# A two-layer graph network: the first layer's output product with node sums stationary, and the second edge sum's products one tile earlier

## The chip, the cores and the metric

The kernel runs on one core of a Trainium2 chip. The metric is the device time of one launch in microseconds (us), the median of several runs. The core has five engines, each with its own instruction queue that runs in order: PE (TensorE, matrix products and transposes into PSUM), DVE (VectorE), ACT (ScalarE), POOL (GpSimd) and SP (SyncE, which only issues DMAs here). They wait for each other through semaphores. PEld in the profile is PE's loading of the stationary operand, which overlaps with products.

## The reference

Inputs: x (128 graphs, 128 nodes, 64 features), adj (128 x 128 x 128, about an eighth of the entries positive, the rest zero), and weights W1 (128 x 192), b1, W2 (192 x 64), b2, W (64 x 64), all float32. Cut to what is computed:

```python
def _L0_gnn_ref(x, adj, W1, b1, W2, b2):
    mask = (adj > 0.0).astype(x.dtype)
    W1a, W1b = (W1[:F], W1[F:])
    xj_proj = x @ W1a
    diff = x[:, :, None, :] - x[:, None, :, :]
    h = jax.nn.relu(xj_proj[:, :, None, :] + diff @ W1b + b1)
    hm = jnp.einsum('bjkh,bjk->bjh', h, mask)
    deg = jnp.sum(mask, axis=-1)
    return hm @ W2 + deg[..., None] * b2

def _L1_gnn_ref(vertices, g_mat, W):
    agg = jnp.einsum('bnm,bmf->bnf', g_mat, vertices)
    return jnp.einsum('bnf,of->bno', agg, W)

h = jnp.maximum(_layernorm(x, axis=-1), 0.0)
x = x + _L0_gnn_ref(h, adj, W1, b1, W2, b2)
h = jnp.maximum(_layernorm(x, axis=-1), 0.0)
return x + _L1_gnn_ref(h, adj, W)
```

For each graph b and node j, hm[j] is the sum over j's neighbours k of relu(A[j] - C[k]), with 192 hidden units. hm @ W2 is the product that the change rewrites.

## The kernel before

**Groups.** The 128 graphs are handled in 32 groups of four (G = 4). In a group, graph b is written as b = 2p + r, p and r in 0 and 1. The first 128 hidden units are "kind 0" (one graph fills the 128 partitions), the other 64 are "kind 1" (two graphs, p = 0 and 1, share the partitions).

**Slots and edges.** A node's neighbours are put into 24 slots (four quarters of the neighbours, six slots each). One-hot matrices S pick the neighbour of a slot, and PE forms A[j] - C[k] for all slots in PSUM (`Job.fill`, tile g). For kind 0, DVE sums absolute values over the slots (tile hm; relu(x) is half of x + |x|, and the linear halves are put in elsewhere). For kind 1, ACT takes the relu (tile T) and POOL adds the slots up. Nodes with more neighbours in a quarter than slots have the rest on a list of up to 128 edges (tiles ov, R, S2, X, RT), which is subtracted or added by `edge_sum` and `edge_sum1`.

**Tiles in time.** A group has T = 24 jobs, called tiles 0 to 23 here, in the hand-written ORDER: 0 to 3 kind 0, 4 and 5 kind 1, 6 to 9 kind 0, 10 and 11 kind 1, and the same once more for r = 1. Products of kind 0 use the whole 128-column array, those of kind 1 use it as two halves of 64 columns. Behind each tile the tables AHEAD, OWN and BEHIND (lines 909 to 936) hang other work: AHEAD is the preparation of group g + 1 (its slots, ranks, the projections pp at tiles 7 and 12, the edge lists), OWN the edge values X, BEHIND the end of group g - 1. Before the change BEHIND reads:

```python
0: (slot_sum,), 1: (edge_sum,), 4: (edge_sum1,), 8: (post0,), 10: (post1,),
15: (post2,), 16: (post3,), 19: (post4,),
```

At one tile BEHIND stands ahead of AHEAD.

**The end of a group.** `slot_sum` adds the two halves of hm0 on POOL (hs). `edge_sum` forms pe0 in PSUM and u0 = hs - pe0 on DVE: u0 is [128 hidden, 4 graphs, 128 nodes]. `edge_sum1` does the same for the other 64 units: two transposes of z1, eight records of products X by RT with 64-column halves, and u1 = hm1 - pe1 on DVE, [2 x 64 hidden, r, 128 nodes]. `post0` multiplies with W2 as the stationary operand, so that the result py has output features on partitions; ACT copies it to ys. `post1` transposes ys back (pty), adds the residual e on DVE to form x1 (the first layer's output, nodes on partitions; the profile calls it x), and takes mean and variance of each graph (four bn_stats and four bn_aggr on DVE, tiles stb and mvb). `post2` is the second layer norm (ACT: square root sdb, four h; DVE: rsb, mrb), `post3` the product with adj (pga, copied to agg by ACT), `post4` the product with W (po), the sum with x1 on DVE (ot) and the store.

**Projections.** `pre_proj` forms pp (float) on PE, and ACT copies it to bf16 (ca<-pp), then writes z (four instructions) and e (two). DVE takes what the rounding left (rest), ACT rounds that (ca<-rest), POOL the last remainder; DMAs then stack the three parts for the next group (k3).

**Edge weights on ACT.** For each group ACT computes R in nine instructions: four et<-iov,mid, four et<-et,half (pre_edge_b), and R itself.

**PSUM.** The tiles g and pp share three buffers of two banks (ps_g), all other products two buffers of one bank (ps_m). A new tile waits for the readers of the tile whose buffer it takes.

**What sets the order.** PE's instructions stay in the order of the program throughout (`mm` and `tp`). For DVE, ACT, POOL and SP only the start of the kernel is held (Engine.held); from group 0 on a scheduler in the tile layer sorts each engine's instructions when the program is built, by its own estimate of when they are ready. The order on each engine is then fixed.

Of the kernel before, what the change touches and what calls it, by code (L numbers as in the profile page):

```python
# [8 lines left out]
F32 = mybir.dt.float32  # L9
BF16 = mybir.dt.bfloat16  # L10
I32 = mybir.dt.int32
AF = mybir.ActivationFunctionType
ALU = mybir.AluOpType
# [137 lines left out]
def kernel(  # L151
# [28 lines left out]
    def mm(*args, **kw):  # L180
        return tc.keep_in_program_order(nc.tensor.matmul(*args, **kw))  # L181

    def tp(*args, **kw):
        return tc.keep_in_program_order(nc.tensor.transpose(*args, **kw))  # L184

    class Engine:
# [4 lines left out]
        def __init__(self, engine):  # L191
            self.engine = engine
# [10 lines left out]
    vec, act, pool, sp = (Engine(e) for e in (nc.vector, nc.scalar, nc.gpsimd, nc.sync))  # L203

    B, N, F = x.shape
    H = W1.shape[1]
    O = W2.shape[1]
    P = 128
    G = 4
# [18 lines left out]
    with ExitStack() as main:  # L228
# [4 lines left out]
        tmp = main.enter_context(tc.tile_pool(name="tmp", bufs=2))  # L233
# [3 lines left out]
        def gtile(name):  # L237
            return ps_g.tile([P, 2, 512], F32, tag="g", name=name)

        def mtile(name):  # L240
            return ps_m.tile([P, 512], F32, tag="m", name=name)
# [7 lines left out]
        w2bd = const.tile([P, 2, O], F32, tag="w2bd", name="w2bd")  # L249
        wl1 = const.tile([P, P], F32, tag="wl1", name="wl1")  # L250
        ident = const.tile([P, P], F32, tag="ident", name="ident")
# [20 lines left out]
        for q in range(Q):  # L272
            s = slice(q * QN, (q + 1) * QN)
# [35 lines left out]
        w2h = const.tile([C0, O], F32, tag="w2h", name="w2h")  # L309
# [69 lines left out]
        def bc(t, n, axis):  # L379
            shape = list(t.shape)  # L380
            shape.insert(axis, n)
            return t.unsqueeze(axis).to_broadcast(shape)
# [37 lines left out]
        def keep_busy(tile, n):  # L420
            for _ in range(n):
                mm(tile, oneb, bc(oneb, 4, 1), start=True, stop=True, skip_group_check=True)

        def pre_adj(g, busy=0):
            d = groups[g]
            pt = mtile(f"pt{g}")
            keep_busy(pt, busy)
            for b in range(G):
                tp(pt[:, b * N : (b + 1) * N], d["adj"][:, b, :], ident)
            d["adjT"] = grp.tile([P, G, N], F32, tag="adjT", name=f"adjT{g}", bufs=3)  # L430
            if g == 0:
                pre_norm(0)
            act.activation(
                d["adjT"].rearrange("k b j -> k (b j)"), pt, AF.Copy
            )
            if g < 2:
                return
            pre_mask(g)
# [11 lines left out]
            d["h"] = tmp.tile([P, 2, 2, F], F32, tag="h", name=f"h{g}", bufs=1)  # L450
            norm_b(d["x"], d["mv"], lambda b: d["h"][:, b % 2, b // 2, :], f"a{g}", d.get("scales"))

        def pre_rank(g, busy=0):
            d = groups[g]
            pq = mtile(f"pq{g}")
            keep_busy(pq, busy)
            mm(
                pq, triq, d["maskT"].rearrange("k b j -> k (b j)"), start=True, stop=True
            )
            d["qs"] = grp.tile([P, G, N], BF16, tag="qs", name=f"qs{g}")  # L460
            qf = d["qs"].rearrange("k b j -> k (b j)")
            act.activation(qf, pq, AF.Copy)

            d["ov"] = grp.tile([P, G, N], BF16, tag="ov", name=f"ov{g}")
            vec.tensor_scalar(d["ov"], d["qs"], float(D) + BIG, None, ALU.is_ge)
# [56 lines left out]
                d["hT"].rearrange("p r n -> p (r n)"), ph[:, 0 : 2 * N], AF.Copy  # L522
            )

        def pre_count(g, busy=0):
            d = groups[g]

            pd = mtile(f"pd{g}")
            keep_busy(pd, busy)
            for b in range(G):  # L530
                mm(
                    pd[:, b : b + 1], d["maskT"][:, b, :], negb, start=True, stop=True
                )
                mm(
                    pd[:, G + b : G + b + 1], d["ov"][:, b, :], oneb[:, 0:1], start=True, stop=True
                )
            d["dn"] = grp.tile([P, 2, G], F32, tag="dn", name=f"dn{g}")
            vec.tensor_copy(d["dn"].rearrange("j t b -> j (t b)"), pd[:, 0 : 2 * G])

            d["ns"] = grp.tile([P, G], F32, tag="ns", name=f"ns{g}")  # L540
            vec.scalar_tensor_tensor(
                d["ns"], pd[:, G : 2 * G], float(Q * D), d["dn"][:, 0], ALU.add, ALU.subtract
            )

            d["half"] = tmp.tile([P, G], F32, tag="half", name=f"half{g}")
            vec.tensor_scalar(
                d["half"], pd[:, G : 2 * G], -0.5, 0.5, ALU.mult, ALU.add
            )
            d["nb"] = tmp.tile([P, G], BF16, tag="nb", name=f"nb{g}")
            vec.tensor_copy(d["nb"], pd[:, G : 2 * G])  # L550
# [197 lines left out]

        def edge_sum1(g):
            d = groups[g]  # L750
            ph = mtile(f"pe1{g}")
            for r in range(2):
                mm(
                    ph[:, r * N : (r + 1) * N], d["z1"][:, r].rearrange("j p u -> j (p u)"), ident,
                    start=r == 0, stop=False, is_transpose=True, skip_group_check=True,
                )
            for b in (0, 2, 1, 3):
                p, r = b // 2, b % 2
                mm(
                    ph[p * C1 : (p + 1) * C1, r * N : (r + 1) * N], d["X"][:, b, C0:H],  # L760
                    d["RT"][:, b, :], start=False, stop=True, skip_group_check=True,
                )
            d["u1"] = tmp.tile([P, 2, N], F32, tag="u1", name=f"u1{g}", bufs=1)
            vec.tensor_tensor(
                d["u1"], d["hm1"], ph[:, 0 : 2 * N].rearrange("h (r j) -> h r j", r=2), ALU.subtract
            )


        def post0(g):
            d = groups[g]  # L770
            py = mtile(f"py{g}")
            d["py"] = py
            for p in range(2):
                s = slice(p * O, (p + 1) * O)
                mm(
                    py[s, 0 : 2 * N], w2h,
                    d["u0"][:, 2 * p : 2 * p + 2].rearrange("h r j -> h (r j)"),
                    start=True, stop=False, skip_group_check=True,
                )
            w = w2bd.rearrange("h p o -> h (p o)")  # L780
            mm(
                py[:, 0 : 2 * N], w, d["u1"].rearrange("h r j -> h (r j)"),
                start=False, stop=True, skip_group_check=True,
            )
            d["ys"] = tmp.tile([P, 2, N], F32, tag="ys", name=f"ys{g}", bufs=1)
            act.activation(
                d["ys"].rearrange("p r j -> p (r j)"), py[:, 0 : 2 * N], AF.Copy
            )

        def post1(g):  # L790
            d = groups[g]
            pt = mtile(f"pty{g}")
            for r in range(2):
                tp(pt[:, r * N : (r + 1) * N], d["ys"][:, r], ident)
            d["x1"] = grp.tile([P, G, F], F32, tag="x1", name=f"x1{g}")
            vec.tensor_tensor(
                d["x1"].rearrange("j (p r) o -> j r p o", p=2),
                pt[:, 0 : 2 * N].rearrange("j (r p o) -> j r p o", r=2, p=2),
                d["e"].rearrange("j (p r) o -> j r p o", p=2),
                ALU.add,  # L800
            )
            d["mv"] = norm_a(d["x1"], f"b{g}")

# [30 lines left out]


        class Job:
            def __init__(self, g, kind, b, jh, qp, busy):
                self.g, self.kind, self.b, self.jh, self.qp = g, kind, b, jh, qp
                self.gt = gtile(f"g{g}_{kind}_{b}_{jh}_{qp}")
                keep_busy(self.gt[:, 0], busy)  # L840

                if kind == 0:
                    self.parts = [(b, slice(0, C0), slice(0, P))]
                else:
                    self.parts = [
                        (2 * p + b, slice(C0, H), slice(p * C1, (p + 1) * C1)) for p in range(2)
                    ]
# [79 lines left out]
        BEHIND = {  # L927
            0: (slot_sum,),
            1: (edge_sum,),
            4: (edge_sum1,),  # L930
            8: (post0,),
            10: (post1,),
            15: (post2,),
            16: (post3,),
            19: (post4,),
# [85 lines left out]
        for g in range(NG):  # L1021
            if 0 < g < NG - 1:
                load(g + 1)
            order = ORDER0 if g == 0 else ORDERL if g == NG - 1 else ORDER
            for t, args in enumerate(order):
                job = Job(g, *args, busy=0)
                job.fill()
                job.drain()
                if g == 0 and t in FIRST:
                    FIRST[t](0)  # L1030
                pieces(OWN, t, g)
                pieces(BEHIND, t, g - 1)
                pieces(AHEAD if g else AHEAD0, t, g + 1)
# [37 lines left out]
```

## Time and profile before

| what | us |
|---|---|
| runs shown: median (lowest to highest) | 972.44 (972.28 to 972.99) |
| the profiled execution: its own time | 972.88 |
| its span, first to last instruction | 971.2 |
| one group in the steady part | 29.13 |
| first rank product of group 1, and of group 31 | 15.2, 903.9 |
| mean granted TensorE clock | 0.994 |

A line of the timeline has start, length, engine, source line, operation, the tiles that it writes and reads by name, their shape, how many instructions are merged in the line, and in brackets how long the engine was idle before it and what ended that. For PE, "128*128" is the stationary operand and "128x256" the moving one or the result; a float product is recorded as two records, a bf16 product as one. Nearly all instructions carry the line of a helper (L181 for products, L184 for transposes, L198 for the other engines), so tiles are found by name.

Some groups of the profile that the change touches (count, busy us in all, mean ns of one):

| engine, tiles | form | count | busy | mean |
|---|---|---|---|---|
| PE py<-u,w2h | 128*64, 256 columns, float | 128 | 20.8 | 404 |
| PE py<-u,w2bd | 128*128, 256 columns, float | 64 | 22.4 | 431 |
| PE pty<-ident,ys | 128*128 transposes | 64 | 13.9 | 299 |
| ACT ys<-py | 128x256 | 32 | 13.5 | 422 |
| DVE x<-pty,e | 128x256 | 32 | 13.3 | 416 |
| DVE stb<-x | 128x64 | 128 | 19.4 | 213 |

### The profile page before, as it was taken

The numbers are of one execution on the slowest core, as the hardware profiler recorded it, in microseconds if no ns is written. First come the engines' busy times: TensorE is split into PE (matmuls) and PEld (weight loads), VectorE is DVE, ScalarE is ACT, GpSimd is POOL, SyncE is SP. The second block draws the span as 40 slices with busy tenths as digits, with TensorE's granted clock in tenths as the row PEclk, the third lists the DMA queues.
The fourth block names the chain that finished last, engine by engine and source line by source line (L and its number), as shares of the span: only waits on it lengthen the run. The fifth ranks groups of instructions, "written<-read, shape, count | busy, mean of one in ns | idle before, by whom it ended". The sixth has DMA issues, their size and how long they took to land. (4 is left out here: it accounts for less than half of the span.)

```text
span 971.2 us, 26764 instructions
## 1 busy us (share of the span) xinstructions
PE 945.9 (97%) x10007; PEld 692.5 (71%) x10008; DVE 796.4 (82%) x1880; ACT 698.9 (72%) x1732; POOL 743.1 (77%) x1130
## 2 busy tenths in 40 slices
PE   6899999999999999999999999999999999999995
PEld 2667777777777767777777777777777777777774
DVE  6788888888888888888888888888888888888863
ACT  4867787767787767787767787767787767787752
POOL 1388787778787778787778787778787778787793
PEclk9999999999999999999999999999999999999998
DMA  3655676655676655676655676655676655666510
GB/s 99 132 128 126 150 166 137 148 128 124 145 165 144 138 127 128 147 163 144 138 128 128 146 163 137 145 129 127 146 164 144 140 126 126 147 154 138 123 46 14
DMA packets 88294, 129.91 MB, mean 134 GB/s; under 512 B 47200, under 2 KB 63968, under 8 KB 88160
## 3 DMA queue, kind: packets, MB, share of 16 engines
q1 hardware_dynamic: 87584, 127.98, 57.8%
q8 instruction: 81, 1.33, 0.6%
q14 instruction: 53, 0.43, 0.1%
q10 hardware_dynamic: 576, 0.16, 0.1%
HBM read 13.01 MB, written 4.19 MB: 18 GB/s over the span
## 5 line engine op out<-in xcount | busy, mean ns | idle before, releaser
L198 POOL TENSOR_TENSOR T<-T 128x192 f32<-128x192 f32 (+2 forms) x768 | 526.3, 692 | 97.2 <-ACT T L198 57.2
L198 DVE TENSOR_REDUCE hm<-g 128x64 f32<-128x768 f32 x512 | 476.8, 947 | 81.2 <-PE g L181 79.5
L181 PEld LDWEIGHTS <-k 96*128 96x128 bf16 (+1 forms) x6144 | 411.0, 103 | 177.1 <-issue 51.3
L181 PE MATMUL g<-S,k 96*128 96x384 bf16 (+1 forms) x2048 | 381.9, 330 | 4.7 <-DVE hm L198 3.5
L181 PE MATMUL g<-id,k 96*128 96x192 bf16 (+1 forms) x4096 | 379.8, 246 | 0.0
L198 ACT ACTIVATE T<-g 128x768 f32<-128x768 f32 x256 | 209.5, 820 | 74.5 <-PE g L181 70.2
L198 POOL TENSOR_TENSOR ca<-rest,ca 128x384 bf16<-128x384 f32 x126 | 112.5, 913 | 103.7 <-ACT ca L198 101.2
L198 ACT ACTIVATE ca<-pp 128x768 bf16<-128x768 f32 x64 | 51.4, 803 | 56.0 <-PE pp L181 56.0
L198 DVE TENSOR_TENSOR rest<-pp,ca 128x768 f32<-128x768 f32 x64 | 60.8, 949 | 14.6 <-ACT e L198 14.0
L198 ACT ACTIVATE ca<-rest 128x768 bf16<-128x768 f32 x64 | 55.2, 862 | 22.2 <-DVE rest L198 22.2
L198 DVE TENSOR_SCALAR S<-qs 128x512 bf16<-128x512 bf16 x186 | 71.0, 434 | 0.0
L181 PE MATMUL pe<-RT,X 128*64 128x128 f32 (+1 forms) x512 | 70.5, 280 | 0.0
L181 PE MATMUL pp<-wp,hT 64*128 64x448 f32 x256 | 67.0, 600 | 0.4 <-DVE bias L198 0.4
L198 ACT ACTIVATE z<-pp,ns 128x128 f32<-128x128 f32 (+1 forms) x256 | 65.9, 348 | 0.0
L198 ACT ACTIVATE et<-et,half 128x128 f32<-128x128 f32 x128 | 57.0, 449 | 0.0
L198 ACT ACTIVATE qs<-pq 128x512 bf16<-128x512 f32 x32 | 19.1, 597 | 52.2 <-PE pq L181 50.4
L181 PEld LDWEIGHTS pe<-RT,X 128*64 128x64 f32 (+1 forms) x512 | 52.7, 165 | 5.4 <-issue 5.4
L181 PE MATMUL px<-ca,S 128*128 128x192 bf16 x384 | 52.7, 246 | 0.0
L181 PE MATMUL px<-ca,R 128*128 128x192 bf16 x384 | 52.6, 246 | 0.0
L198 ACT ACTIVATE h<-x,mrb,rsb 128x64 f32<-128x64 f32 x128 | 51.6, 478 | 1.0 <-DVE mrb L198 1.0
L198 ACT ACTIVATE h<-x,mra,rsa 128x64 f32<-128x64 f32 x128 | 48.6, 432 | 1.8 <-issue 1.3
L181 PE MATMUL pe<-ident,z 128*128 128x128 f32 x192 | 49.6, 286 | 0.0
(128 smaller groups left out, 1208.3 us busy)
## 6 DMA issues: line engine op xcount, KB each, us to landing
S<-S SPq DMA_DIRECT2D x372, 192.0 KB, 4.1
k<-ca SPq DMA_DIRECT2D x384, 96.0 KB, 2.2
adj<-in_adj_dram SPq DMA_DIRECT2D x32, 256.0 KB, 3.0
x<-in_x_dram SPq DMA_DIRECT2D x32, 128.0 KB, 2.7
out_dram<-ot SPq DMA_DIRECT2D x32, 128.0 KB, 2.2
w<-in_L_gnn_W_dram SPq DMA_DIRECT2D x2, 96.0 KB, 4.5
bias<-in_L_gnn_b_dram ACTq DMA_DIRECT2D x1, 96.0 KB, 3.5
w2a<-in_L_gnn_W_dram ACTq DMA_DIRECT2D x1, 32.0 KB, 2.3
```

The lines of the kernel that those rows point to most:

```text
L181: return tc.keep_in_program_order(nc.tensor.matmul(*args, **kw))
L198: ins = f(*args, **kw)
```

## The change

The first layer's output product is turned round. `post0` makes u0[:, b] (128 hidden by 128 nodes of graph b) the stationary operand and streams the 64 columns of W2's first part (w2h): four products. It then makes u1[:, r] stationary and streams w2bd, W2's other 64 rows laid out twice as a block diagonal, 128 columns for p = 0 and 1: two products that add to the same PSUM tile. The result py has nodes on partitions and [b, o] along the row. The copy ys and the transposes pty are gone; `post1` adds e straight from py, and moves from behind tile 10 to behind tile 8, right after `post0`.

`edge_sum1` is cut in two. Its products go behind tile 3 (before: tile 4); the subtraction that forms u1 becomes `edge_sum2`, behind tile 4.

The argument busy of `pre_adj`, `pre_rank`, `pre_count` and `Job`, which was 0 in all calls, is removed with its calls of keep_busy.

```diff
 def edge_sum1(g):
     d = groups[g]
-    ph = mtile(f"pe1{g}")
+    ph = d["pe1"] = mtile(f"pe1{g}")
...
+
+def edge_sum2(g):
+    d = groups[g]
+    ph = d["pe1"]
     d["u1"] = tmp.tile([P, 2, N], F32, tag="u1", name=f"u1{g}", bufs=1)
     vec.tensor_tensor(
         d["u1"], d["hm1"], ph[:, 0 : 2 * N].rearrange("h (r j) -> h r j", r=2), ALU.subtract
...
 def post0(g):
     d = groups[g]
-    py = mtile(f"py{g}")
-    d["py"] = py
-    for p in range(2):
-        s = slice(p * O, (p + 1) * O)
-        mm(
-            py[s, 0 : 2 * N], w2h,
-            d["u0"][:, 2 * p : 2 * p + 2].rearrange("h r j -> h (r j)"),
-            start=True, stop=False, skip_group_check=True,
-        )
-    w = w2bd.rearrange("h p o -> h (p o)")
-    mm(
-        py[:, 0 : 2 * N], w, d["u1"].rearrange("h r j -> h (r j)"),
-        start=False, stop=True, skip_group_check=True,
-    )
-    d["ys"] = tmp.tile([P, 2, N], F32, tag="ys", name=f"ys{g}", bufs=1)
-    act.activation(
-        d["ys"].rearrange("p r j -> p (r j)"), py[:, 0 : 2 * N], AF.Copy
-    )
+    py = d["py"] = mtile(f"py{g}")
+    for b in range(G):
+        mm(
+            py[:, b * O : (b + 1) * O], d["u0"][:, b], w2h,
+            start=b == 0, stop=False, skip_group_check=True,
+        )
+    pyr = py[:, 0 : G * O].rearrange("j (p r o) -> j r p o", p=2, r=2)
+    for r in range(2):
+        mm(
+            pyr[:, r], d["u1"][:, r], w2bd, start=False, stop=True, skip_group_check=True,
+        )

 def post1(g):
     d = groups[g]
-    pt = mtile(f"pty{g}")
-    for r in range(2):
-        tp(pt[:, r * N : (r + 1) * N], d["ys"][:, r], ident)
     d["x1"] = grp.tile([P, G, F], F32, tag="x1", name=f"x1{g}")
     vec.tensor_tensor(
-        d["x1"].rearrange("j (p r) o -> j r p o", p=2),
-        pt[:, 0 : 2 * N].rearrange("j (r p o) -> j r p o", r=2, p=2),
-        d["e"].rearrange("j (p r) o -> j r p o", p=2),
-        ALU.add,
+        d["x1"], d["py"][:, 0 : G * O].rearrange("j (b o) -> j b o", b=G), d["e"], ALU.add
     )
     d["mv"] = norm_a(d["x1"], f"b{g}")
...
 BEHIND = {
     0: (slot_sum,),
     1: (edge_sum,),
-    4: (edge_sum1,),
-    8: (post0,),
-    10: (post1,),
+    3: (edge_sum1,),
+    4: (edge_sum2,),
+    8: (post0, post1),
     15: (post2,),
```

More of the change, by code (lines that the diff above doesn't have):

```diff
@@ L422, in keep_busy, with pre_adj @@
                 mm(tile, oneb, bc(oneb, 4, 1), start=True, stop=True, skip_group_check=True)
-        def pre_adj(g, busy=0):
+        def pre_adj(g):
             d = groups[g]
             pt = mtile(f"pt{g}")
-            keep_busy(pt, busy)
             for b in range(G):
@@ L451, in pre_norm, with pre_rank @@
             norm_b(d["x"], d["mv"], lambda b: d["h"][:, b % 2, b // 2, :], f"a{g}", d.get("scales"))
-        def pre_rank(g, busy=0):
+        def pre_rank(g):
             d = groups[g]
             pq = mtile(f"pq{g}")
-            keep_busy(pq, busy)
             mm(
@@ L523, in pre_hT, with pre_count @@
             )
-        def pre_count(g, busy=0):
+        def pre_count(g):
             d = groups[g]
             pd = mtile(f"pd{g}")
-            keep_busy(pd, busy)
             for b in range(G):
@@ L836, with __init__ @@
         class Job:
-            def __init__(self, g, kind, b, jh, qp, busy):
+            def __init__(self, g, kind, b, jh, qp):
                 self.g, self.kind, self.b, self.jh, self.qp = g, kind, b, jh, qp
                 self.gt = gtile(f"g{g}_{kind}_{b}_{jh}_{qp}")
-                keep_busy(self.gt[:, 0], busy)
                 if kind == 0:
@@ L1025 @@
             for t, args in enumerate(order):
-                job = Job(g, *args, busy=0)
+                job = Job(g, *args)
                 job.fill()
```

## The prediction

> **What bounds the kernel now.** I read the page first, then busy time by stretch, then PE's and ACT's timelines of one group side by side.
>
> ```profile
> PE 945.9 (97%) x10007; PEld 692.5 (71%) x10008; DVE 796.4 (82%) x1880; ACT 698.9 (72%) x1732; POOL 743.1 (77%) x1130
> ```
>
> ```profile
> 485.00:514.13 29.13, 29.05 (x316) 21.42 (x312) 24.52 (x58) 21.69 (x56) 23.23 (x36) 1.00 0.61 138
> 514.13:543.26 29.13, 29.05 (x316) 21.43 (x312) 24.50 (x58) 21.68 (x56) 23.21 (x36) 1.00 0.63 144
> ```
>
> The second fence holds two stretches of one group each (busy us of PE, weight load, DVE, ACT, POOL, then granted clock): every group takes 29.13 us at full clock, PE looks full and ACT a quarter idle. That reading is what I distrust. A matmul's recorded time covers its pipeline, so the time a product costs is the distance from its start to the next start. Tile 18 to tile 20 of group 16, on PE and on ACT (start, length):
>
> ```profile
> 516.01 0.49 PE L181 MATMUL g<-id,k 96*128 96x192 bf16 x4
> 516.40 0.48 PE L181 MATMUL g<-S,k 96*128 96x384 bf16 x2
> 516.73 0.49 PE L181 MATMUL g<-id,k 96*128 96x192 bf16 x4
> 517.06 0.64 PE L181 MATMUL po<-wl1t,agg 128*128 128x128 f32 x4
> 517.67 0.48 PE L181 MATMUL g<-S,k 96*128 96x384 bf16 x2
> ```
>
> ```profile
> 506.53 0.84 ACT L198 ACTIVATE ca<-rest 128x768 bf16<-128x768 f32 x1 [0.75 <-DVE rest L198]
> 507.28 0.79 ACT L198 ACTIVATE T<-g 128x768 f32<-128x768 f32 x1
> ...
> 515.19 0.46 ACT L198 ACTIVATE et<-et,half 128x128 f32<-128x128 f32 x1
> 515.48 0.87 ACT L198 ACTIVATE T<-g 128x768 f32<-128x768 f32 x1
> 516.17 0.45 ACT L198 ACTIVATE agg<-pga 128x256 f32<-128x256 f32 x1
> 516.44 0.48 ACT L198 ACTIVATE et<-et,half 128x128 f32<-128x128 f32 x1
> 516.73 0.89 ACT L198 ACTIVATE T<-g 128x768 f32<-128x768 f32 x1
> 517.42 0.48 ACT L198 ACTIVATE et<-et,half 128x128 f32<-128x128 f32 x1
> 517.71 0.38 ACT L198 ACTIVATE sda<-mva,eps 128x4 f32<-128x4 f32 x1
> 517.94 0.76 ACT L198 ACTIVATE R<-et,ones 128x512 bf16<-128x512 f32 x1
> ```
>
> The four po products need 4 x 0.11 = 0.45 us (the same shape steps by 0.11 in pt<-ident,adj: 0.44 for four), but tile 20 starts 0.61 after them: 517.67, which is 0.05 after the second T ended (516.73 + 0.89 = 517.62). Tile 19 starts 516.40, 0.05 after the first T's end (515.48 + 0.87). I followed this through the trace: in 28 groups running, tile 20 starts 50 to 52 ns after that T ends. The built program has exactly these waits: tile 19's first product waits for tile 16's T, tile 20's for tile 17's, because they reuse those PSUM buffers. And ACT has no idle time at all from 506.53 to 518.70. So PE does not set the period: the chain is PE to the end of pp at 503.25, ACT ca/z/e to 505.51, DVE rest (505.54, 0.96 us), ACT ca at 506.53, then 10.2 us of ACT in order up to T at 516.73, then PE from tile 20 to the next group's pp. ACT's idle quarter lies outside this stretch. The waits table hides it, since PE's waits of 0.14 us fall inside recorded matmul time.
>
> The Trainium skill (Perfetto Trace Analysis, Identifying the Most-Contended Engine) says that matmul busy share is a poor measure of how near TensorE is to its limit, and weight-load share a better one; the 71% beside the 97%, and the 0.14 us wait inside "busy" time, agree. By matmul share every PE saving would be time; by the chain none is unless it lies before pp.
>
> **The change, part by part.**
>
> *pe1 behind tile 3.* Before, its products stand between tiles 4 and 5, which use 64-column halves of the array, and PE changes shape three times (128 to 64 to 128 to 64). A change costs 0.10: products of g<-id step by 0.08, but 0.18 ahead of a tile of the other width. From the end of tile 3's products (498.09) to tile 5 (499.82), less tile 4 (0.68), pe1 costs 1.05. Behind tile 3 the two transposes follow a 128-column tile (0.11 + 0.11), one change (0.10), the eight products as now (499.33 to 499.82: 0.49), and tile 4 follows without a change: 0.80. Gain 0.25, with a rounding's worth at tile 5: **0.27**, all ahead of pp, so all on the chain. T of tile 4 comes 0.6 later on ACT, which is idle there (1.11 us before it). The subtraction u1 stays at tile 4 in DVE's order.
>
> *py with sums stationary.* Old py: 504.01 to 505.13 plus 0.10 of shape change = 1.21. New: six float products, each two records: 8 records of 64 columns, 4 of 128. The 128-column ones: 4 x 0.11 = 0.45. For the 64-column ones, no row of the steady part has the form. Lower bound 0.055: half the columns of 0.11, and a float 128x128 load (z) already hides behind a bf16 product of 0.055 in pe0. Upper bound 0.11: the pe<-RT,X step with the same stationary size and twice the columns. I take 0.06 (nearest to the z row). py costs 0.93 (0.90 to 1.35). The Trainium skill (TensorE: Matmul & The Clock Gate, LDWEIGHTS) puts a load at columns / 1.2 ns, 107 ns for 128, and denies float the fast load; by it eight loads would take 0.86 and py 1.3, a loss on PE. The z row says 0.055, and I follow the row. Either way py is behind pp, where PE has time: between tiles 11 and 20 it will wait.
>
> *No transposes back, no ys.* pty took 506.69 to 507.06 plus 0.10: 0.47 of PE gone. ys (0.43) leaves ACT, but it stood in ACT's wait for rest (0.75 idle behind it), so the chain gains nothing from it.
>
> *x and its statistics two tiles earlier.* The built program's order puts x on DVE between tile 8's reduction and rest. x now waits directly for py; queued behind it are rest, the four bn_stats and four bn_aggr, tile 9's reduction, and through rest ACT's ca, PE's tile 11. With tile 8's reduction shifted to 503.85 and py starting 503.65, py ends 504.58, its result comes 0.20 later (the last record's 0.31 from start), x runs 504.78 to 505.20 and rest can start with e's end at 505.24 + 0.03 = 505.27. So x is hidden in DVE's wait for e (0.46 before). That cover holds until py costs about 1.09; at 1.35 rest is 0.26 late. The statistics go behind rest, in front of tile 9's reduction; pp of r=1 waits for that reduction (507.9) and would start at 508.6 anyway.
>
> *What the diff does not show: ACT's order.* With x early, the scheduler has re-sorted ACT. Before, between ca<-rest and T of tile 17 stand three of the four et<-et,half; R and the fourth come after T. In the new program all four, and R, stand ahead of T of tile 17. An et<-et,half steps by 0.29 (515.19 to 515.48). R steps by 0.62 where something follows at once (0.61 and 0.63, two places at the start). Also h of the second norm stands in front of ca<-pp: it needs mrb, which needs sdb. sdb would start 509.57 and end 509.85, rsb to 510.07, mrb from 510.10; mrb took 0.51 (0.16 where POOL was idle, at the end of the run), so h starts between 510.34 (when ACT is free: no idle) and 510.64. I take 0.23 of idle, mrb ending with the POOL instruction beside it, as it does now; bounds 0 and 0.31.
>
> *Sum for one group*: -0.27 + 0.29 + 0.62 + 0.23 = **+0.87**, period 30.00. The PE savings (0.28 + 0.47) become longer waits before tiles 11, 12, 19 and 20. Thirty groups (1 to 30) have both post and pre work: +26.1. In group 31 nothing of pre is left on ACT and some of PE's 1.0 counts: -0.5 (0 to -1.0). At the end, where everything is a chain, x starts at 960.08, 2.0 after u1 ended (958.06); new, eight records from 957.79 and four more, each 0.06 to 0.21 there (po's step 0.21 at the end), give x at 959.1 to 959.8: -0.6. Profiled execution: 972.88 (span 971.2 and 1.7 around it) + 25.0 = 997.9; the median shown is 0.44 lower, so **997.5**.
>
> **Rivals.**
> - *PE is what counts (chance 0.10).* It speaks for it that PE is 97% busy and DVE and ACT are seen waiting for PE g (79.5 and 70.2 us in all). Then 0.27 + 0.28 + 0.47 = 1.0 a group goes, 31 times: about 941; 954 with py at its upper bound. It speaks against it that tiles 19 and 20 start 0.05 after an ACT end, in 28 groups, while the waited-for instructions are in the new chain too. It decides if R and the et's turn out to run in idle ACT time, that is if T of tile 17 ends earlier than 517.6 by this group's clock.
> - *Loads do not hide (0.17).* As forecast, but the 64-column records cost 0.11: x ends 505.6, rest and all of the ACT chain 0.26 later: 30 x 1.13 = 33.9, about 1005.
> - *A draw (0.04).* ACT's extra is 0.29 only, R being covered: +0.02 a group, 972. Against it: ACT is in order and R is ahead of T.
> - That the change does not do what it says is excluded for PE: in the built order pty and ys are gone and pe1 stands ahead of tile 4.
>
> **How the numbers follow.** Forecast 0.69, rivals as above. The forecast's own bounds: no idle for mrb and all of the small gains, 0.64 x 30 - 2.0: 990; idle 0.31 and py 1.35, 1.21 x 30 - 0.3: 1008. Range 987 to 1008; below it lies little but the PE rival. About 0.2% (2 us) is what a measurement of this kernel can tell from no change: faster 0.10, same 0.03, slower 0.87.
>
> **What would show it.** Right: group period near 30.0; T of tile 17 about 1 us later against pp's end (15.6 from pp's end to tile 20, against 14.4) and tile 20 still 0.05 behind it; ACT with no gap from ca<-rest to T except one before h; a step of 0.6 or more behind po; tile 12 waiting for T. py about 0.9, pe1 0.8. Wrong: period 28.1 with PE steps unbroken (then R was hidden), or x later than e's end on DVE (then the loads cost).

## The result and the profile after

| what | us |
|---|---|
| before, median (lowest to highest) | 972.72 (972.28 to 973.87) |
| changed, median (lowest to highest) | 1016.00 (1013.72 to 1017.20) |
| changed / before, 95% interval | 1.044 (1.0419 to 1.0461) |
| changed, the profiled execution and its span | 1017.2, 1015.4 |
| one group in the steady part: before, changed | 29.13, 30.69 |

The kernel became 4.4% slower. The forecast had the direction and 25 of the 43 us: 997.5, range 987 to 1008. Busy time of each engine over the span, after:

```profile
PE 932.9 (92%) x10135; PEld 719.4 (71%) x10136; DVE 789.5 (78%) x1880; ACT 689.2 (68%) x1700; POOL 734.8 (72%) x1130
```

PE, DVE, ACT and POOL all have less to do than before (PE 945.9, ACT 698.9), and the span is 44 us longer: what was added is waiting. Two stretches of one group each (length, then busy us of PE, weight load, DVE, ACT, POOL):

```profile
485.30:515.99 30.69, 28.65 (x317) 22.07 (x315) 24.36 (x57) 21.41 (x54) 22.96 (x36) 1.00 0.60 134
515.99:546.68 30.69, 28.84 (x322) 22.46 (x320) 24.32 (x57) 21.41 (x54) 22.96 (x36) 1.00 0.60 135
```

The clock is as before (1.00), so the 1.56 us a group are not PE running slower. The changed kernel's timeline of ACT, from `ca<-rest` of r=0 to `T` of tile 17:

```profile
528.32 0.84 ACT L198 ACTIVATE ca<-rest 128x768 bf16<-128x768 f32 x1 [1.31 <-DVE rest L198]
...
531.80 0.68 ACT L198 ACTIVATE et<-et,half 128x128 f32<-128x128 f32 x2
532.69 0.44 ACT L198 ACTIVATE h<-x,mrb,rsb 128x64 f32<-128x64 f32 x1 [0.21 <-DVE mrb L198]
...
537.58 0.75 ACT L198 ACTIVATE et<-et,half 128x128 f32<-128x128 f32 x2
538.16 0.87 ACT L198 ACTIVATE T<-g 128x768 f32<-128x768 f32 x1
538.85 0.45 ACT L198 ACTIVATE agg<-pga 128x256 f32<-128x256 f32 x1
539.12 0.80 ACT L198 ACTIVATE R<-et,ones 128x512 bf16<-128x512 f32 x1
539.73 0.88 ACT L198 ACTIVATE T<-g 128x768 f32<-128x768 f32 x1
```

and its timeline of PE around tile 20:

```profile
539.73 0.64 PE L181 MATMUL po<-wl1t,agg 128*128 128x128 f32 x4
540.66 0.48 PE L181 MATMUL g<-S,k 96*128 96x384 bf16 x2 [0.29 <-ACT T L198]
```

R now stands ahead of T of tile 17 and steps by 0.61 (539.12 to 539.73), `h` waits 0.21 for mrb, and tile 20 (540.66) starts 0.05 after that T's end (539.73 + 0.88 = 540.61). The waits table has PE's wait for a T of ACT at 92 places (tiles 12, 19 and 20 of each group), where it had two before:

```profile
PE g L181 <- ACT T L198: 49.4, 92, 0.7
...
PEld ph L184 <- DVE u L198: 18.1, 30, 0.7
```

The second line (8.7 us in 30 waits before) was not in the forecast. PE's timeline of the same group, at pe1 and at py, and DVE's lines behind py:

```profile
519.87 0.38 PE L181 MATMUL pe<-ident,z 128*128 128x128 f32 x2
520.18 0.66 PE L181 MATMUL pe<-RT,X 128*64 128x128 f32 x8
520.67 0.50 PE L181 MATMUL g<-S,k 96*64 96x384 bf16 x4
...
525.42 1.03 PE L181 MATMUL py<-w2h,u 128*128 128x64 f32 x8
526.29 0.66 PE L181 MATMUL py<-w2bd,u 128*128 128x128 f32 x4
526.79 0.49 PE L181 MATMUL g<-S,k 96*128 96x384 bf16 x2
```

```profile
526.99 0.42 DVE L198 TENSOR_TENSOR x<-py,e 128x256 f32<-128x256 f32 x1 [0.41 <-PE py L181]
527.33 0.95 DVE L198 TENSOR_TENSOR rest<-pp,ca 128x768 f32<-128x768 f32 x1
```

pe1 takes 0.80 (519.87 to 520.67), as worked out. py takes 1.37 (525.42 to 526.79), and its eight 64-column records 0.87, which is 0.11 each and not 0.06. x waits for it, and rest, queued behind x, starts 0.32 after e ended (526.46 + 0.55 = 527.01).

With the chain cut into legs (medians over 24 steady groups, worked out from the traces), the whole difference can be laid out. Pp's end is taken as the start of the product behind it. The last two columns are the first two experiments:

| leg, us | before | changed | R put back | only the split |
|---|---|---|---|---|
| end of pp to end of e (ACT) | 2.26 | 2.25 | 2.25 | 2.25 |
| end of e to rest (DVE) | 0.03 | 0.32 | 0.32 | 0.03 |
| rest to ca<-rest (ACT) | 0.99 | 0.98 | 0.98 | 0.99 |
| ca<-rest to end of T of tile 17 | 11.08 | 12.30 | 11.40 | 11.07 |
| that end to tile 20 (PE) | 0.05 | 0.05 | 0.05 | 0.05 |
| tile 20 to the next pp's end | 14.72 | 14.78 | 14.36 | 14.45 |
| period | 29.13 | 30.69 | 29.37 | 28.84 |

Forecast were 0, 1.14 and -0.27 for the second, fourth and sixth leg. They came out as 0.29, 1.22 and +0.06.

### The profile page after: what moved, and what is told of

Same layout as the page of the kernel before. It is cut to its first block, busy times and chain, and to the rows that moved or that the text cites. A ratio compares the mean times of both kernels' runs of the same rounds, so it can differ in the third digit from the quotient of the medians.

```text
span 1015.4 us, 26958 instructions
## 1 busy us (share of the span) xinstructions
PE 932.9 (92%) x10135; PEld 719.4 (71%) x10136; DVE 789.5 (78%) x1880; ACT 689.2 (68%) x1700; POOL 734.8 (72%) x1130
## 4 chain that ended last, share of the span: by engine, by line
PE 58%; ACT 23%; DVE 11%; issue 6%; POOL 1%; DMA 0%; SPq 0%; ACTq 0%; POOLq 0%; DVEq 0%
PE g L181 31%; ACT T L198 9%; PE pp L181 6%; PE px L181 6%; PE py L181 4%; ACT h L198 4%; DVE maskT L198 3%; PE pe L181 3%; DVE rest L198 3%; ACT et L198 2%; DVE u L198 2%; ACT R L198 2%; ACT X L198 2%; PE pga L181 2%; ACT adjT L198 1%
## 5 line engine op out<-in xcount | busy, mean ns | idle before, releaser
L198 POOL TENSOR_TENSOR T<-T 128x192 f32<-128x192 f32 (+2 forms) x768 | 518.6, 682 | 149.0 <-ACT T L198 109.1
L181 PEld LDWEIGHTS <-k 96*128 96x128 bf16 (+1 forms) x6144 | 418.0, 104 | 212.4 <-issue 98.8
L198 ACT ACTIVATE T<-g 128x768 f32<-128x768 f32 x256 | 203.3, 820 | 73.5 <-PE g L181 73.4
L198 ACT ACTIVATE h<-x,mrb,rsb 128x64 f32<-128x64 f32 x128 | 55.0, 471 | 6.8 <-DVE mrb L198 6.8
L198 DVE TENSOR_SCALAR maskT<-adjT 128x512 bf16<-128x512 f32 x32 | 33.4, 1044 | 22.9 <-ACT adjT L198 22.8
L198 POOL TENSOR_TENSOR hm<-T 128x64 f32<-128x64 f32 x128 | 40.7, 318 | 9.9
```

Source lines behind the costliest of these rows:

```text
L198: ins = f(*args, **kw)
```

## The experiments

In the diffs `behind(a, b)` is an order without a wait: the scheduler must put a after b on their common engine. T17 is the activation T of tile 17, hm9 the reduction of tile 9, and so on. The diffs are shortened; orders that only hold an instruction where it already stood are left out. Each ratio is to the kernel before, run on the same chip, with its 95% interval. Periods are medians of the steady groups.

**1. R put back behind T of tile 17.**

```diff
 for b in range(G):
-    act.activation(
+    ins = act.activation(
         d["et"][:, b, :], d["et"][:, b, :], AF.Relu, bias=d["half"][:, b : b + 1]
     )
+    if b >= 2: behind(ins, agg if b == 2 else T17)
...
-act.activation(d["R"], d["et"], AF.Relu, bias=ones[:, 0:1], scale=-1.0)
+behind(act.activation(d["R"], d["et"], AF.Relu, bias=ones[:, 0:1], scale=-1.0), T17)
+behind(sda, T17)
```

> The changed kernel with one thing put back: on ACT, R, sda and the last et<-et,half stand behind T of tile 17 again (the third between agg and that T), as before the change; PE, DVE, py and pe1 stay as changed. If the chain through ACT to T of tile 17 sets the period, the chain loses R (0.61) and one et<-et,half (0.29): period 30.69 - 0.90 = 29.79, 30 groups, about 1016 - 27 = 989. If ACT's order is without weight, and the loss comes from py's loads and the late x alone, 1016 (period 30.69). If tile 20 then waits for something else next (rest late, tile 19's T), something between: 995 to 1005.

Measured: 983.32, ratio 1.0093 (1.0073 to 1.0113), period 29.37. The leg on ACT fell by 0.90, as expected, so ACT's order does set the time. But the leg from tile 20 to the next pp fell as well, by 0.42, which the expectation did not have. All of it is at one place, ph's wait for u at tile 1; every other step of PE there is the same to 0.01. PE's two lines there, in a group of the changed kernel, of this run and of the kernel before:

```profile
548.72 0.49 PE L181 MATMUL g<-id,k 96*128 96x192 bf16 x4
549.62 0.44 PE L184 MATMUL ph<-ident,h 128*128 128x128 f32 x2 [0.41 <-DVE u L198]
```

```profile
529.87 0.49 PE L181 MATMUL g<-id,k 96*128 96x192 bf16 x4
530.34 0.44 PE L184 MATMUL ph<-ident,h 128*128 128x128 f32 x2
```

```profile
525.73 0.49 PE L181 MATMUL g<-id,k 96*128 96x192 bf16 x4
526.30 0.44 PE L184 MATMUL ph<-ident,h 128*128 128x128 f32 x2
```

The step from the one to the other is 0.90, 0.47 and 0.57.

**2. Only edge_sum1 cut in two.**

```diff
-            4: (edge_sum1,),
+            3: (edge_sum1,),
+            4: (edge_sum2,),
```

> The kernel before with only edge_sum1 cut in two, its products behind tile 3; py, the transposes back and the order on ACT and DVE are as before. If the shape change saved (0.27 a group, all ahead of pp) is on the chain, 972.7 - 30 x 0.27 = 964.6, period 28.86. If it is eaten wherever it is made, by tile 0 waiting for k3's DMAs and by ph waiting for u0 as in the changed kernel (where tile 20 to the next pp took 14.79 against 14.72 before), 972 to 975, period 29.1 to 29.2. If it is eaten only because the changed kernel delays POOL and ACT, 964.6.

Measured: 964.62, ratio 0.9905 (0.9883 to 0.9926). Two stretches of one group each:

```profile
433.74:462.59 28.85, 28.77 (x316) 21.48 (x314) 23.81 (x58) 21.56 (x54) 23.11 (x36) 1.00 0.62 143
462.59:491.43 28.84, 28.77 (x316) 21.47 (x314) 23.81 (x58) 21.56 (x54) 23.11 (x36) 1.00 0.63 143
```

The last leg is 0.28 shorter, the 0.27 of the forecast, and all of it arrives in the time. This half of the change is a gain by itself. In the whole change it is lost again at ph.

**3. R, the last et and sda ahead of T of tile 17 in the kernel before.**

```diff
-            19: (pre_edge_b,),
+            16: (pre_edge_b,),
+behind(T17, R)
```

> The kernel before with only ACT's order changed: the last et<-et,half, sda and R stand ahead of T of tile 17 instead of behind it; the products are all as before. If ACT's chain to that T sets the period: 0.29 + 0.22 + 0.62 = 1.13 a group, 30 groups, 972.7 + 34 = 1006.6, period 30.26. If ACT has room there and PE's products set the period, 972.7. If the late PE stream gives some of it back ahead of the next pp (RT and S2 come no later than before), 995 to 1006.

Measured: 1006.06, ratio 1.0334 (1.0311 to 1.0356), period 30.37. The number is the one expected, and the way to it is not: tile 20 started before T of tile 17 had ended. The tile layer assigns the three PSUM buffers by its own schedule; with T of tile 17 later, it gave tile 20 the buffer of tile 18 (reader: DVE) and tile 21 that of tile 17. And on DVE the scheduler had put rsa, which waits for sda, ahead of tile 18's reduction. Besides, ph's step grew by 0.35, to 0.92. A time that fits is not yet a mechanism that fits. The run was made once more without sda:

**4. The same with sda behind T of tile 17.**

```diff
+behind(sda, T17)
```

> The kernel before with R and the last et<-et,half ahead of T of tile 17 on ACT, sda behind that T as before, and DVE's order as before (in the run with sda ahead as well, DVE's rsa waited for sda ahead of tile 18's reduction, so tile 20 waited for DVE, and the time, though near the one expected, came about in another way). If ACT's chain to T of tile 17 sets the period: 0.29 + 0.62 = 0.91 a group, 972.7 + 27.3 = 1000, period 30.04, tile 20 starting 0.05 behind the end of T of tile 17. If moving R also brings the longer wait of ph for u (0.43 more in the changed kernel than with its R put back), period 30.4 to 30.5, 1010 to 1014. If ACT has room, 972.7.

Measured: 968.44, ratio 0.9956 (0.994 to 0.9973), period 28.96: faster than before, against all three cases (0.10 of the 0.17 that it gains a group is ph's step, 0.47 here). ACT, PE and DVE around tile 20 (516.39):

```profile
516.06 0.72 ACT L198 ACTIVATE R<-et,ones 128x512 bf16<-128x512 f32 x1
516.69 0.79 ACT L198 ACTIVATE T<-g 128x768 f32<-128x768 f32 x1
```

```profile
516.39 0.49 PE L181 MATMUL g<-S,k 96*128 96x384 bf16 x2
```

```profile
515.38 0.96 DVE L198 TENSOR_REDUCE hm<-g 128x64 f32<-128x768 f32 x1 [1.94 <-PE g L181]
```

Tile 20 starts 0.05 after tile 18's reduction (515.38 + 0.96 = 516.34) and 0.30 before T of tile 17 even begins. R stands ahead of that T here too, and costs nothing. So an instruction ahead of that T costs what tile 20's wait for it makes of it, and this wait belongs to a buffer that the planner chose, not to the computation. My expectation had taken the buffers as given. In the changed kernel itself another buffer for tile 20 was not tried.

**5. What a load costs.** Blocks of eight products on constants in one group of the changed kernel, results unused.

```diff
+run("qfa", lambda i: [(f4[i % 4], w2h, {})])
+run("qfb", lambda i: [(f4[i % 4], w2h[:, 0:32], {})])
+run("qfe", lambda i: [(f4[i % 4][:, 0:64], w2h, {})])
...
+run("qta", lambda i: [(f4[i % 4], ident, flip), (b4[i % 4], oneb, {})])
+run("qtb", lambda i: [(f4[i % 4], w2h, {}), (b4[i % 4], oneb, {})])
```

> The changed kernel with ten blocks of products put once into group 16, behind tile 23, on constants, results unused: blocks of eight, start-to-start step of a record. If a float 128x128 load does not hide, the step is the same for 32, 64 and 128 moving columns, 0.11 (full clock). If columns set it, 0.027 to 0.03 for 32, 0.055 for 64, 0.11 for 128. Float 64-column stationary by 64: 0.055 if the load scales with its columns, 0.11 if not. bf16 by 64 and by 128: 0.027 to 0.055, or a bound of its own. A float transpose in turn with a bf16 product of 128 columns, as z in pe0: 0.11 + 0.055 for a pair if z's load hides behind the product; the same for a plain float product by 64 in turn with a bf16 product tells if it was the transpose or the neighbour that hid it. Time near 1016 + 10.

Measured: 1032.98 in one run. Steps from start to start of one record, at full clock:

| block | stationary, moving | step, ns |
|---|---|---|
| qfa | float 128x128, 64 columns | 112 |
| qfb | float 128x128, 32 columns | 112 |
| qfd | float 128x128, 192 columns | 163 |
| qfe | float 128x64, 64 columns | 58 |
| qba | bf16 128x128, 64 columns | 29 |
| qbb | bf16 128x128, 128 columns | 56 |
| qta | float transpose (one record), bf16 128 columns, in turn | 115, 56 |
| qtb | float 64 columns (two records), bf16 128 columns, in turn | 112, 112, 56 |

PE's timeline at three of the blocks; a float product of one line has two records, so the distance between lines is two steps:

```profile
545.08 0.39 PE L181 MATMUL qfa<-w2h,upper 128*128 128x64 f32 x2
545.30 0.39 PE L181 MATMUL qfa<-w2h,wl1t 128*128 128x64 f32 x2
...
554.53 0.28 PE L181 MATMUL qfe<-w2h,ones 128*64 128x64 f32 x2
554.65 0.28 PE L181 MATMUL qfe<-w2h,upper 128*64 128x64 f32 x2
...
557.79 0.39 PE L181 MATMUL qtb<-w2h,ones 128*128 128x64 f32 x2
558.01 0.22 PE L181 MATMUL qtb<-oneb 128*128 128x128 bf16 x1
558.07 0.39 PE L181 MATMUL qtb<-w2h,upper 128*128 128x64 f32 x2
```

The step of a float product is 112 whether 64 or 32 columns move, and about half (58) when the stationary operand is half as wide: at these few moving columns the load sets the step. It does so beside a bf16 product too (qtb). The rule of the Trainium skill (TensorE: Matmul & The Clock Gate, LDWEIGHTS), columns / 1.2 ns, gives 107; measured 112.

**6. maskT from PSUM.** The runs so far left ph's wait for u. On DVE maskT stands ahead of u, and it lasts 0.73 on average before, 1.04 in the changed kernel, 0.47 with R put back. DVE and the POOL instruction beside it, in one group of the changed kernel, and of the run with R put back:

```profile
547.01 1.09 DVE L198 TENSOR_SCALAR maskT<-adjT 128x512 bf16<-128x512 f32 x1 [0.80 <-ACT adjT L198]
...
546.82 1.00 POOL L198 TENSOR_TENSOR T<-T 128x384 f32<-128x384 f32 x1
```

```profile
528.17 0.43 DVE L198 TENSOR_SCALAR maskT<-adjT 128x512 bf16<-128x512 f32 x1 [0.81 <-ACT adjT L198]
...
527.26 0.99 POOL L198 TENSOR_TENSOR T<-T 128x384 f32<-128x384 f32 x1
```

maskT ends 0.28 (548.10 against 547.82) and 0.35 (528.60 against 528.25) after POOL's instruction, however long it had been waiting: a wait, recorded as duration. The traces of the kernel before and of run 3 say the same: maskT lasts 0.76 and 1.17 there (medians over 24 steady groups), and ends 0.28 after POOL's instruction in both. The test lets it read the PSUM tile instead of ACT's copy in SBUF:

```diff
-    vec.tensor_scalar(d["maskT"], d["adjT"], 0.0, -1.0, ALU.is_gt, ALU.mult)
+    src = pt.rearrange("k (b j) -> k b j", b=G)
+    vec.tensor_scalar(d["maskT"], src, 0.0, -1.0, ALU.is_gt, ALU.mult)
```

> The changed kernel with one input changed: DVE's maskT reads PSUM (tile pt) in place of ACT's copy adjT in SBUF; the order on all engines stays. In the changed kernel maskT takes 1.09 in the steady groups against 0.43 in the run with R put back, each time ending 0.28 to 0.34 behind the end of the POOL instruction that ran as it started, and ph waits 0.43 longer for u. If maskT waits for POOL because both read SBUF, maskT falls to 0.5 to 0.7, starts about 0.7 earlier (pt is there before adjT), and ph's wait falls by 0.43: 1016 - 13 = 1003, period 30.26. If the 0.43 comes from hs, or from u being late for another reason, 1016 and ph still waits.

Measured: 1006.18, ratio 1.0349 (1.0332 to 1.0367), period 30.30, the last leg 14.38.

```profile
541.33 0.69 DVE L198 TENSOR_SCALAR maskT<-pt 128x512 bf16<-128x512 f32 x1 [0.80 <-ACT adjT L198]
...
541.14 1.00 POOL L198 TENSOR_TENSOR T<-T 128x384 f32<-128x384 f32 x1
```

It starts at the same point of the group (the earlier start that was expected did not come, since the built program still lets it wait for adjT), beside the same POOL instruction, and ends 0.12 before that one does. The 0.40 that the group gained is this wait. The Trainium skill (SBUF — State Buffer, SBUF: two separate sides) says that a GpSimd instruction and a VectorE instruction in a two-port mode, or with two SBUF inputs, take a shared pair of SBUF ports by an exclusive lock, held for a whole instruction, and that the one that comes second is blocked until then. The three groups of lines agree with such a lock; no row names the mode that maskT runs in.

**7. x behind rest as well** (on top of run 6).

```diff
+behind(x, rest)
```

> The changed kernel with maskT from PSUM (1006.2 us, period 30.29) and x behind rest on DVE instead of ahead of it; R and all four et<-et,half stay ahead of T of tile 17. There rest starts 0.32 behind the end of e, since x waits for py. If py's loads cost the time through this place alone: -0.29 a group, period 30.00, 1006.2 - 8.7 = 997.5; with h's wait for mrb (0.21) gone as well, 29.8, 991. If x's place on DVE is without weight, 1006. If tile 12, which then waits for the reduction of tile 9 behind x, takes its place, 1003 to 1006.

Measured: 991.46, ratio 1.0196 (1.0172 to 1.0219), period 29.83. The second leg is back at 0.03 (from 0.32), and h no longer waits (the scheduler moved sdb ahead of et<-iov,mid by itself): 0.29 and 0.19 in the legs. R and the four et's are still ahead of T of tile 17 here: the leg on ACT is 1.04 longer than before (12.12 against 11.08), of which run 1 puts 0.90 down to them. The last leg is 0.34 shorter than before, and 0.70 a group is left of the loss.

**8 to 12. A version that beats both.** pre_edge_a behind tile 7, so that et<-iov,mid fill ACT's wait for rest; R, sda and the last et behind T of tile 17; x behind rest; all h behind e of r=1.

```diff
-            7: (lambda g: pre_proj(g, 0),),
-            9: (pre_edge_a,),
+            7: (lambda g: pre_proj(g, 0), pre_edge_a),
```

> The changed kernel with ACT's order set by hand: pre_edge_a behind tile 7, so that the four et<-iov,mid (1.17) fill ACT's wait for rest; x behind rest on DVE; all h of the second norm behind e of r=1; the last et<-et,half, sda and R behind T of tile 17. If the ACT chain sets the period, it loses 1.0 (iov), 0.29 (late x) and 0.21 (h waiting for mrb) against 29.36 with only R put back, which is below what PE's products need without waits: the changed kernel's 30.69 less its waits (0.57 for ph, 0.80, 0.76 and 0.46 ahead of tiles 11, 12, 19 and 20 and two of 0.08) is 27.9. So PE sets it then: period 27.9 to 28.2, 972.7 - 30 x 1.1 = 940 (935 to 950). If tile 11's wait for rest stays as long as it is (0.8), 28.7, 960.

Measured: 952.09, ratio 0.979 (0.9768 to 0.9813), period 28.47, which is 0.27 above the upper end of what was expected. Tile 20 now starts 0.60 after T of tile 17 ended, with no wait in front: PE sets it there. Tile 12 still waited, for tile 9's reduction, which stood behind x. With the old py in the same order:

> The same order on ACT as in the run above, but with the old py, ys and the transposes back (x on DVE where it was before), and edge_sum1 cut in two: what the new py is worth once ACT does not set the period. PE's products are then longer by 0.47 (pty) and shorter by 0.16 (old py 1.21 against the new 1.37): period 28.2 to 28.5, 972.7 - 30 x 0.75 = 950 (944 to 956), 9 above the run above. If ACT's ys or the late x cost as well, 955 to 962; if the form of py is without weight, equal to the run above.

Measured: 985.37, ratio 1.0134 (1.0117 to 1.0152), period 29.54. This says nothing of py: the scheduler had put ys behind ca<-rest on ACT, and PE's first transpose back waited 0.94 for it. Then x behind tile 9's reduction, and maskT from PSUM:

```diff
-            8: (post0, post1),
+            8: (post0,),
+            9: (post1,),
+behind(x, hm9)
```

> As the run with pre_edge_a at tile 7 (952.1 us, period 28.47), with x behind the reduction of tile 9 on DVE, and maskT from PSUM. There tile 12 waited 0.32 for that reduction, which stood behind rest and x, and ph 0.10 for u. If PE's products set the rest: period 28.05, 952.1 - 12.6 = 939.5 (937 to 945). If another wait takes the place (pp of r=1 for T of tile 10, sdb for mvb), 945 to 952.

Measured: 948.01, ratio 0.9748 (0.9728 to 0.9769), period 28.33. Two terms were too large: 0.10 of tile 12's wait was the change of array shape, and tile 15 now waited 0.13. The old py once more, with pre_edge_a at tile 8, so that ys stays ahead of ca<-rest:

> The old py, ys and the transposes back, with edge_sum1 cut in two, ys ahead of the et<-iov,mid on ACT (in the first try with the old py, ys stood behind ca<-rest, and the transposes waited 1.0 for it), maskT from PSUM, the rest of ACT's order as in the run above. PE then has 0.47 more for the transposes and 0.16 less for py: period 0.31 longer than in the run above, about 9 us above it, 949 (945 to 955). If ACT's fourth et<-iov,mid behind ca<-rest makes T of tile 17 late, 955. If the two come out equal, the new form of py is without worth even where PE sets the period.

Measured on the same chip: 956.23 (954.0 to 957.0, against 946.9 to 950.8 for the run above), ratio 0.9829 (0.9807 to 0.985), period 28.53. So once PE sets the time, the new form of py and the transposes it saves are worth 0.20 a group in the steady part, and 8 us in all (of 0.31 worked out; 0.13 is tile 15's wait, which the run with the old py does not have). The two also differ in where pre_edge_a and x stand, but PE's steps away from py, the transposes and tile 15 are the same in both to 0.03. Last, the next group's statistics moved into DVE's idle time:

```diff
+behind(sta, hm15)
```

> As the run with x behind the reduction of tile 9 (948.0 us, period 28.33), with the next group's statistics sta and mva behind the reduction of tile 15 on DVE, where DVE was idle for 1.9, instead of between tile 12's and tile 13's reductions. There tile 15 waited 0.13 for tile 13's reduction, the last wait of PE in a group that is above 0.03 and not a change of shape. If PE's products alone set the period: 28.20, 948.0 - 30 x 0.13 = 944 (942 to 946). If rest of r=1 or tile 17 becomes late in its place, 948.

Measured: 946.91, ratio 0.9745 (0.9731 to 0.9759): 2.5% below before and 69 us below the change. Its busy time, and two stretches of one group each:

```profile
PE 921.8 (98%) x10136; PEld 708.9 (75%) x10136; DVE 778.9 (82%) x1880; ACT 682.6 (72%) x1700; POOL 732.2 (77%) x1130
```

```profile
397.46:425.66 28.20, 28.19 (x320) 21.95 (x318) 23.94 (x58) 21.18 (x53) 22.87 (x36) 1.00 0.64 146
425.66:453.86 28.20, 28.19 (x320) 21.95 (x318) 23.93 (x58) 21.18 (x53) 22.88 (x36) 1.00 0.64 146
```

The period is the 28.20 expected. In seven of the groups from 23 on it is 28.3 to 28.7: tile 0 then waits, for k3's DMAs by the waits table. That is why 946.9 and not 944; it was not tried further.

## Why the prediction was right and where it was wrong

- **The chain.** Right. Tile 20 starts 0.05 behind T of tile 17 in the steady groups, PE's savings became waits (0.76 before tile 19, 0.46 before tile 20), and putting R and one et back removed 0.90. The PE rival (941 or 954) was wrong. But the link is weaker than I wrote: run 4 shows that it is a choice of buffer.
- **ACT's additions**, 0.29 + 0.62 + 0.23. Right, a little small: 0.29, 0.61, 0.21. The leg grew by 1.22, 0.11 more than these: the et just ahead of h's wait takes its whole length (531.80 + 0.68 = 532.48) and not the step of 0.29 that it takes where an instruction follows at once.
- **py's records: the step that failed.** "I take 0.06 (nearest to the z row)" was 0.11. The z row could not give this price: the 0.055 is the step of the bf16 product ahead of z, and z's own step is 0.11, with 128 moving columns. In run 5 a plain float product, too, starts 0.056 behind a bf16 product; what it costs stands behind it, 0.112 for each of its two records, with 64 moving columns or 32. The rule of the Trainium skill that I weighed and set aside (107 ns for 128 columns) was right, and so was the rival "loads do not hide" in its mechanism and its size: rest 0.29 later (it said 0.26). Run 7 takes this term out (and h's 0.19 with it, which the legs keep apart). It is worth 30 x 0.29 = 9 us.
- **pe1 behind tile 3**, "all ahead of pp, so all on the chain". Right alone (0.28 in run 2), wrong in the sum. I let each saving on the chain pass to its end. But R and the et ahead of T of tile 17 put POOL's work 0.90 earlier against tile 20 (in the trace, POOL's T additions start 1.54 before tile 20, and 0.64 before it with R put back). That set another POOL instruction beside maskT, and u and ph came late: the leg from tile 20 to pp is 0.06 longer instead of 0.27 shorter. This is the second step that failed, 30 x 0.33 = 10 us.
- Together: these two and 0.08 more on ACT make the 30.00 that was forecast into 30.69, and 997.5 into 997.5 + 30 x 0.69 = 1018. Measured 1016.0; the 2 us between lie outside the steady groups and were not broken down.
- **The range.** Its upper end took py at 1.35 and mrb at its worst, 1008. It had no term for a wait that shows as duration; I saw that mrb took 0.16 without POOL and 0.51 beside it, and did not ask which other DVE instruction would meet POOL at another point.

## What to carry to other kernels

When a product is turned round so that fewer columns move, price it by the load of its stationary operand, from a row of the same kind (a float product that moves as few columns, by the step behind it), and look at what is queued behind its result. Where a scheduler or a planner sits between the source and the engines, an edit moves order and buffers elsewhere: compare the built orders, find which instruction each wait belongs to, and pin the few that matter; here the same py and pe1, with the order pinned, three pieces of other work moved (pre_edge_a, x, the statistics) and maskT read from PSUM, are 2.5% faster instead of 4.4% slower. Most of that is not py's: with the old py, and the statistics where they were, it is 1.7%. When VectorE and GpSimd both work from SBUF, ask of a shift in time not only what is late, but which pairs of instructions now meet.

## What was unexpected in the hardware

- A wait of VectorE for GpSimd is booked as busy time: the same maskT lasts 0.43 (R put back), 0.76 (before) or 1.09 (changed), according to when POOL's instruction ends.
- Behind products that move few columns for each load the clock fell, although PE shows no idle time. The blocks qfa and qfb of run 5 (64 and 32 columns a load) ran from 544.63 to 548.22, and the block after them was granted half:

```profile
546.40:548.20 1.80, 1.80 (x18) 1.80 (x18) 0.00 (x0) 0.33 (x2) 1.64 (x4) 0.98 0.03 9
548.20:551.67 3.47, 3.47 (x18) 3.47 (x18) 0.00 (x0) 0.00 (x0) 1.74 (x4) 0.52 0.00 0
```

  The third number from the end is the granted clock, 0.52; that block (128 columns, float) stepped by 0.21. Whether the few columns were the cause was not tried by itself.
